# Queueing the state-space scan's decay exponentials behind the attention's score exponentials on ScalarE

## The chip, the cores and the metric

The kernel runs on one core of one Trainium2 chip. The metric is the device time of one execution in microseconds (us). A core has five engines that work side by side, each through its own queue and in that queue's order: TensorE (PE in the profile; PEld is its weight load), VectorE (DVE), ScalarE (ACT), GpSimd (POOL) and SyncE (SP), which here issues the DMAs.

## The reference, cut to what matters

Four residual steps follow one another for each of four batches of 512 rows. The first is a state-space block (a scan over 512 positions for 512 channels with 16 states each), the second a quantised gated feed-forward, the third a cross attention with 16 heads and 512 keys, the fourth four small experts.

```python
def step(state, xs):                                   # the scan, over positions
    d_t, B_t, C_t, u_t = xs
    dA = jnp.exp(d_t[..., None] * A)                   # 512 channels x 16 states
    state = state * dA + (d_t * u_t)[..., None] * B_t[:, None, :]
    y_t = jnp.einsum('ben,bn->be', state, C_t)
    return (state, y_t)
...
scores = jnp.einsum('bqhd,bkhd->bhqk', q, k) * scale   # the attention
attn = jax.nn.softmax(scores, axis=-1)
out = jnp.einsum('bhqk,bkhd->bqhd', attn, v)
...
x = x + jnp.tanh(g_xattn[0]) * _L0_xattn_ref(ctx_1024, _layernorm(x), ...)   # state-space block
x = x + jnp.tanh(g_ffn[0]) * _L0_ffn_ref(_layernorm(x), ...)                 # feed-forward
x = x + jnp.tanh(g_xattn[1]) * _L1_xattn_ref(_layernorm(x), ctx_1024, ...)   # attention
x = x + jnp.tanh(g_ffn[1]) * _L1_ffn_ref(_layernorm(x), ...)                 # experts
```

## The kernel before, in words

**Two streams.** Batch 0 runs its state-space block and its feed-forward alone. After that the kernel gives out two streams side by side: the attention of batch b, head by head, and `layer0(b + 1)`, which is the state-space block (`scan`) and then the feed-forward (`bitnet`) of the next batch. The main loop (L1300 to L1341) has ten slots for each head. In every slot it gives out a piece of the attention of up to three neighbouring heads; and it adds 0.5 to a counter while the scan is being given out (0.8 in the feed-forward), and gives out one piece of `layer0` whenever the counter passes one. So one head goes with five pieces of the scan. `LEADS` says how many heads before its own attention the `layer0` of a batch starts: 16 for batch 1, 17 for batches 2 and 3.

**The scan.** For one batch it has two halves (t0 = 0 and 2), each with 16 states n, each with two channel tiles t: 64 steps. One step is:

- ScalarE writes `dA`, the exponential of delta times A, into a PSUM tile (L652). The tile is one of four in the pool `pss`; two of the four are the accumulators `py` of this half, so two are left for `dA`.
- GpSimd multiplies `du` by `bc`, the row of B that a DMA (L646) has spread over the partitions, into `h` (L186). It does not need `dA`.
- VectorE scans over the positions (L659) and, in six of eight steps, multiplies by `cc` (L660); in the other two VectorE scans (L662) and GpSimd multiplies.
- TensorE adds `h` into `py` by four transposing matmuls (L627).

A piece of the scan is the two steps of one n. At n = 4 of the first half `scan` stands still until `finish(b - 2)` has been given out, because the tile for x of batch b is one of two (L637 to L640).

**The attention.** Each head and each of its four row blocks has scores `ps` (TensorE, L252), their maximum `nmx` (VectorE, L951), its scaling (ScalarE, L963, with `rqs` from GpSimd), and the exponential `pr` (ScalarE, L971). `softmax` gives out two of these exponentials at a time and keeps the last in `mark[0]`; `hl`, the transposed `pT` and the weighted sum `pav` come after it.

**Who sets the order.** When the program is built, a scheduler puts the instructions of each engine in the order in which they will be queued. It takes, by its own estimate of times, the earliest given out of those that are ready. `tc.issue_after(ins)` adds an edge of order: instructions given out inside it are queued behind `ins` on the same engine. It adds no semaphore. The kernel has it already around the staging of weights (`filler`, L1204).

**Where the exponentials stand.** There are 256 score exponentials and 256 exponentials of delta A, each kind in the order given out. Following the loops gives, for each exponential of delta A, how many score exponentials had been given out before it. The table sets this beside the times at which the trace has them (start, us):

| batch, half, n, t | score exponentials given out | it ran at | the last of those ran at |
|---|---|---|---|
| 1, first, 4, 0 | 10 | 397.9 | 396.9 |
| 1, second, 0, 0 | 22 | 477.9 | 513.4 |
| 1, second, 15, 1 | 34 | 577.2 | 589.2 |
| 2, first, 3, 1 | 58 | 759.2 | 749.9 |
| 2, first, 4, 0 | 68 | 762.6 | 812.4 |
| 2, second, 0, 0 | 80 | 866.4 | 895.6 |
| 2, second, 15, 1 | 92 | 957.3 | 973.4 |
| 3, first, 3, 1 | 122 | 1143.2 | 1198.3 |
| 3, first, 4, 0 | 132 | 1144.3 | 1239.1 |
| 3, first, 15, 1 | 140 | 1206.8 | 1295.9 |
| 3, second, 0, 0 | 144 | 1286.6 | 1318.6 |
| 3, second, 15, 1 | 156 | 1372.2 | 1393.0 |

In the trace 168 of the 192 exponentials of delta A of batches 1 to 3 run ahead of the score exponential named in the third column: 47 of batch 1, 57 of batch 2, 64 of batch 3. Score exponentials 1 to 64 are the attention of batch 0, 65 to 128 that of batch 1, and so on.

Of the kernel before, what the change touches and what calls it, by code (L numbers as in the profile page):

```python
# [34 lines left out]
AF = mybir.ActivationFunctionType  # L35
# [75 lines left out]
def flamingo_kernel(  # L111
# [8 lines left out]
    nc = tc.nc  # L120
# [11 lines left out]
    def psum(pool, name, tag="m", bufs=None):  # L132
        if tag == "a":
            role = name.rstrip("_0123456789")
            if pool is psa and role in LAST_PSS and name[len(role)] == str(B - 1):
                return psum(pss, name)
            tag = ATAG.get(role, "m")
            bufs = ABUF[tag]
        kw = {} if bufs is None else {"bufs": bufs}
        return pool.tile([P, 512], F32, tag=tag, name=name, **kw)  # L140
# [12 lines left out]
    def midt(shape, dtype, name, tag):  # L153
        if tag in wider:
            pool, bufs = wider[tag]
            return pool.tile(shape, dtype, tag=f"m{tag}", name=name, bufs=bufs)
        return mid.tile(shape, dtype, tag=tag, name=name, bufs=MIDS[tag])
# [19 lines left out]
    def load_x(b):  # L177
        x_sb[b] = xpool.tile([P, T, L], F32, tag="x", name=f"x{b}", bufs=2)
        nc.sync.dma_start(x_sb[b], x[b].rearrange("(p t) f -> p t f", t=T))
# [5 lines left out]
    def pool_mult(out, a, b):  # L185
        nc.gpsimd.tensor_tensor(out, a, b, ALU.mult)  # L186

    def row_stats(xr, name, gain=1.0, res=None):

        st = sm(6, f"bst{name[0]}", f"bst{name}", 2)  # L190
        nc.vector.bn_stats(st, xr)
        mv = sm(2, f"mv{name[0]}", f"mv{name}")
        nc.vector.bn_aggr(mv, st)
        var = sm(1, f"var{name[0]}", f"var{name}")
        nc.vector.tensor_scalar(var, mv[:, 1:2], EPS, gain**-2, ALU.add, ALU.mult)
        if res is None:
            res = sm(2, f"rst{name[0]}", f"rst{name}")
        rsqrt(res[:, 0:1], var)
        nc.vector.scalar_tensor_tensor(res[:, 1:2], mv[:, 0:1], -1.0, res[:, 0:1], ALU.mult, ALU.mult)
        return res  # L200

    def normed(xr, stats, name, tag="v"):
        xn = midt([P, L], F32, f"xn{name}", tag)
        if name[0] in NRMD:
            nc.vector.tensor_scalar(xn, xr, stats[:, 0:1], stats[:, 1:2], ALU.mult, ALU.add)
        else:
            nc.scalar.activation(xn, xr, AF.Identity, bias=stats[:, 1:2], scale=stats[:, 0:1])
        return xn
# [275 lines left out]
    A = const.tile([P, T, DS], F32, name="A")  # L484
# [30 lines left out]
    def transposed(pool, src, name, g=None):  # L515

        ps = psum(pool, name).rearrange("p (t e) -> p t e", t=T)
        for t, s in enumerate(src):
            nc.tensor.transpose(ps[:, t, :], s[:, g::T], ident)
        return ps[:, : len(src), :]  # L520
# [85 lines left out]
    def scan(b, of_8=DVE_OF_8, G=2, y_tile=lambda name: psum(pss, name), between=lambda n, ins: None):  # L606
        delta, du, ud_d, bd = fronts[b]
        sz_d = dram.tile([P, T, L], F32, tag="szd", name=f"szd{b}", bufs=2)

        def silu_z(t):  # L610

            xt = x_sb[b]
            w = normed(xt[:, t, :], row_stats(xt[:, t, :], f"z{b}{t}", 0.5), f"z{b}{t}")
            th = midt([P, L], F32, f"zth{b}{t}", "t")
            nc.scalar.activation(th, w, AF.Tanh)
            nc.vector.scalar_tensor_tensor(w, th, 1.0, w, ALU.add, ALU.mult)
            return w

        for t0 in range(0, T, G):
            gs = T // G
            ys = [y_tile(f"py{b}{t0}{i}").rearrange("p (g t e) -> p g t e", g=gs, t=G) for i in range(G)]

            def add(src, t, first, last):
                for g in range(T):
                    nc.tensor.matmul(  # L627
                        ys[g // gs][:, g % gs, t, :], src[:, g::T], ident, is_transpose=True,
                        start=first and t == 0 and g % gs == 0, stop=last, skip_group_check=True,
                    )  # L630

            uds, szs = [], []
            for t in range(G):
                uds.append(midt([P, L], F32, f"udr{b}{t0}{t}", "t"))
                nc.sync.dma_start(uds[t], ud_d[:, t0 + t, :])
            for n in range(DS):
                if n == 4 and x_sb[b] is None:  # L637
                    while b >= 2 and estats[b - 2] is None:
                        yield
                    load_x(b)  # L640
                if n == SZR and t0 > 0:
                    for t in range(t0, t0 + G):
                        szs.append(midt([P, L], F32, f"szr{b}{t}", "v"))
                        nc.sync.dma_start(szs[-1], sz_d[:, t, :])
                bc = midt([P, L], F32, f"bc{b}{t0}_{n}", "g")
                nc.sync.dma_start(bc, bd[n, :].partition_broadcast(P))  # L646
                cc = midt([P, L], F32, f"cc{b}{t0}_{n}", "g")
                nc.sync.dma_start(cc, bd[DS + n, :].partition_broadcast(P))
                for t in range(G):
                    nm = f"{b}{t0}{t}_{n}"  # L650
                    dA = psum(pss, f"dA{nm}")
                    last = nc.scalar.activation(  # L652
                        dA, delta[t0 + t], AF.Exp, scale=A[:, t0 + t, n : n + 1]
                    )
                    h = midt([P, L], F32, f"h{nm}", "v")
                    pool_mult(h, du[t0 + t], bc)

                    if (G * n + t) % 8 in of_8:
                        nc.vector.tensor_tensor_scan(dA, dA, h, 0.0, ALU.mult, ALU.add)  # L659
                        nc.vector.tensor_tensor(h, dA, cc, ALU.mult)  # L660
                    else:
                        nc.vector.tensor_tensor_scan(h, dA, h, 0.0, ALU.mult, ALU.add)  # L662
                        pool_mult(h, h, cc)
                    add(h, t, n == 0, n == DS - 1)
                    if n == 2:
                        add(uds[t], t, False, False)
                between(n, last.ins)
                yield

            xt = x_sb[b]  # L670
            if t0 == 0:
                szs = [silu_z(t) for t in range(T)]
                for t in range(G, T):
                    nc.sync.dma_start(sz_d[:, t, :], szs[t])
            for g in range(T):
                if g % gs == 0:
                    acc = midt([P, gs, G, P], F32, f"acc{b}{t0}{g}", "t")
                    nc.scalar.copy(acc, ys[g // gs])
                ps = transposed(pss, szs[:G], f"psz{b}{t0}{g}", g)
                a = acc[:, g % gs]  # L680
                nc.vector.tensor_tensor(a, a, ps, ALU.mult)
                xv = xt[:, g, :].rearrange("q (p e) -> q p e", e=T)[:, :, t0 : t0 + G]
                nc.vector.scalar_tensor_tensor(
                    xv, a.rearrange("q e p -> q p e"), tg[:, 0:1], xv, ALU.mult, ALU.add
                )
                yield
# [511 lines left out]
    mark = [None]  # L1198
# [10 lines left out]
    with tc.tile_pool(name="pro", bufs=1) as pro, tc.tile_pool(name="psp", bufs=4, space=PSUM) as psp:  # L1209
# [26 lines left out]
        def between(n, ins):  # L1236

            if n < 0:
                for _ in range(4):
                    next(side)  # L1240
            for _ in range(2 if 0 <= n < SIDE1 else 0):
                with tc.issue_after(ins):
                    next(side, None)

        run(front(0, inp, between))
        run(scan(0, range(7), 4, iter_ps, between))
        wider.clear()
        for _ in side:
# [34 lines left out]
    def layer0(b):  # L1283

        in_bitnet[0] = False
        if b == 1:
            yield from front(1)
        yield from scan(b)
        in_bitnet[0] = True
        nxt = front(b + 1) if b + 1 < B else iter(())  # L1290
        for k, _ in enumerate(bitnet(b)):
            yield
            if k % NEXT == NEXT - 1:
                next(nxt, None)
        for _ in nxt:
            yield


    n = B * NH
# [114 lines left out]
```

## Time and profile before

| what | value |
|---|---|
| three runs | 2026.92, 2029.95, 2033.11 us; median 2029.95 us |
| the profiled execution | 2033.82 us, its span 2032.0 us |
| granted TensorE clock, mean over the span | 0.877 |
| busy in the span | PE 1634.5, DVE 1536.9, ACT 1328.6, POOL 937.3 us |
| exponentials of delta A, batch 1 | first half 370.0 to 458.0, second 477.9 to 577.2 us |
| batch 2 | first half 737.6 to 831.0, second 866.4 to 957.3 us |
| batch 3 | first half 1118.1 to 1206.8, second 1286.6 to 1372.2 us |
| feed-forward of batches 1, 2, 3: last addition to x (L802) | 747.7, 1132.5, 1528.5 us |
| attention of batches 0 to 3: first and last score exponential | 340.8 to 788.8, 802.3 to 1230.9, 1233.5 to 1590.3, 1602.4 to 1967.7 us |

The times in the table are starts of instructions in one profiled execution, from the start of its span. Busy time is the time in which an engine had work; no engine is busy all the time, and which one is full changes from stretch to stretch. The three runs lie within 6.2 us of each other.

### The profile page before, as it was taken

The page shows a single profiled execution, that of the slowest core. Times are in us where ns is not written, and L with a number is a line of the kernel's source. Part 1 is how long each engine was busy: PE and PEld are TensorE (multiplying, and loading weights), DVE is VectorE, ACT ScalarE, POOL GpSimd, SP SyncE. Part 2 cuts the span into 40 slices and gives each one's busy share as a digit, 9 for nine tenths or more (in the row PEclk, how much of TensorE's full clock was granted, in tenths as well). Part 3 has the DMA queues.
Part 4 walks back from the last instruction along what each step waited for, and adds up shares of the span by engine and source line. Part 5 has one row for each costly group of instructions (what it writes and reads, how often), then busy time and mean ns, then how long its engine had stood idle before and what let it go on. Part 6 is the DMA issues. An engine that isn't in the chain of part 4 may idle for free. (4 is left out here: it accounts for less than half of the span.)

```text
span 2032.0 us, 27171 instructions
## 1 busy us (share of the span) xinstructions
PE 1634.5 (80%) x8366; PEld 901.1 (44%) x8366; DVE 1536.9 (76%) x2893; ACT 1328.6 (65%) x3121; POOL 937.3 (46%) x931
## 2 busy tenths in 40 slices
PE   4354976667879986779898887788999879798888
PEld 1343322344544444455443554554444445454456
DVE  4898865998998787898986885999764564654654
ACT  5797566765757886465658664756565676766763
POOL 1886112784744268475414782775133431412211
PEclk8555987768889998899999989899999889898989
DMA  7553558687884588775435777676445686866754
GB/s 258 185 161 133 151 158 242 185 228 218 231 214 107 132 216 182 191 177 155 106 87 149 199 180 191 156 170 146 91 103 111 139 228 158 210 160 165 193 138 140
DMA packets 516322, 342.50 MB, mean 169 GB/s; under 512 B 425800, under 2 KB 427976, under 8 KB 510032
## 3 DMA queue, kind: packets, MB, share of 16 engines
q1 hardware_dynamic: 516176, 340.77, 64.2%
q8 instruction: 65, 1.06, 0.2%
q14 instruction: 81, 0.66, 0.1%
HBM read 193.10 MB, written 44.30 MB: 117 GB/s over the span
## 5 line engine op out<-in xcount | busy, mean ns | idle before, releaser
L186 POOL TENSOR_TENSOR h<-u,bc 128x512 f32<-128x512 f32 x256 | 334.7, 1327 | 94.5 <-DMA bc<-bd 43.8
L627 PE MATMUL py<-ident,h 128*128 128x128 f32 x1024 | 201.1, 341 | 123.7 <-DVE h L660 101.9
L252 PE MATMUL ps<-kT,qT 128*128 128x512 f16 x768 | 217.0, 406 | 66.5 <-ACT pr L971 51.9
L652 ACT ACTIVATE dA<-delta,A 128x512 f32<-128x512 f32 x256 | 172.6, 685 | 138.8 <-DVE h L660 103.0
L659 DVE TENSOR_TENSOR_SCAN dA<-dA,h 128x512 f32<-128x512 f32 x200 | 240.8, 1217 | 23.5 <-POOL h L186 15.0
L252 PE MATMUL pav<-pT,v 128*128 128x256 f16 x1536 | 215.7, 297 | 46.2 <-DMA pT<-hl 28.9
L627 PEld LDWEIGHTS py<-ident,h 128*128 128x128 f32 x1024 | 167.6, 214 | 167.7 <-DVE h L660 131.0
L951 DVE TENSOR_REDUCE nmx<-ps 128x1 f32<-128x512 f32 x256 | 172.2, 679 | 54.9 <-PE ps L252 54.6
L971 ACT ACTIVATE pr<-ps,nmx,rqs 128x512 f32<-128x512 f32 x256 | 197.7, 775 | 20.8 <-DVE hl L992 16.6
L992 DVE SCALAR_TENSOR_TENSOR hl<-pr,den,hl 128x512 f16<-128x512 f32 x214 | 185.2, 882 | 33.4 <-ACT hl L989 17.0
L252 PEld LDWEIGHTS <-v 128*128 128x128 f16 x1536 | 161.7, 106 | 103.2 <-issue 44.2
L252 PE MATMUL pq<-axnT,wq 128*128 128x512 f16 x768 | 194.1, 404 | 7.7 <-DMA axnT<-xsa 3.1
L252 PE MATMUL pwo<-wo,oT 128*128 128x512 f16 x768 | 181.1, 386 | 8.6 <-DVE oT L244 3.6
L991 POOL TENSOR_SCALAR hl<-pr,den 128x512 f16<-128x512 f32 x86 | 66.3, 771 | 203.5 <-issue 97.5
L252 PEld LDWEIGHTS <-qT 128*128 128x128 f16 x768 | 77.8, 104 | 156.4 <-issue 88.6
L183 POOL TENSOR_TENSOR rqs<-ssq,mhalf 128x4 f32<-128x4 f32 x64 | 68.4, 1068 | 161.9 <-ACT ssq L940 149.0
L252 PEld LDWEIGHTS <-cT 128*128 128x128 f16 x768 | 79.1, 106 | 128.8 <-issue 61.7
L660 DVE TENSOR_TENSOR h<-dA,cc 128x512 f32<-128x512 f32 x200 | 133.7, 677 | 2.5 <-PE py L627 0.5
L252 PEld LDWEIGHTS <-wq 128*128 128x128 f16 x768 | 80.1, 105 | 108.3 <-issue 36.0
L252 PE MATMUL pk<-wk,cT 128*128 128x512 f16 x384 | 110.1, 432 | 19.9 <-DMA wk<-dwk 11.9
L252 PEld LDWEIGHTS <-oT 128*128 128x128 f16 x768 | 74.8, 100 | 100.6 <-issue 10.6
L989 ACT ACTIVATE hl<-pr,den 128x512 f16<-128x512 f32 x128 | 91.8, 717 | 36.3 <-DVE den L978 28.6
(386 smaller groups left out, 3478.2 us busy)
## 6 DMA issues: line engine op xcount, KB each, us to landing
bc<-bd SPq DMA_DIRECT2D x112, 256.0 KB
cc<-bd SPq DMA_DIRECT2D x112, 256.0 KB
wq<-dwq SPq DMA_DIRECT2D x64, 256.0 KB
wo<-dwo SPq DMA_DIRECT2D x64, 256.0 KB
w<-w3d SPq DMA_DIRECT2D x12, 1024.0 KB
de<-hle SPq DMA_DIRECT2D x9, 1024.0 KB
lw<-de SPq DMA_DIRECT2D x18, 512.0 KB
wk<-dwk SPq DMA_DIRECT2D x16, 512.0 KB
```

Of the source, the lines that this page charges most:

```text
L183: nc.gpsimd.tensor_tensor(res, arg, mhalf[:, : arg.shape[1]], ALU.pow)
L186: nc.gpsimd.tensor_tensor(out, a, b, ALU.mult)
L252: nc.tensor.matmul(ps, l, r, start=first and i == 0, stop=last and i == n - 1)
L627: nc.tensor.matmul(ys[g // gs][:, g % gs, t, :], src[:, g::T], ident, is_transpose=True, start=first and t == 0 and g % gs == 0, stop=last ...
L652: last = nc.scalar.activation(dA, delta[t0 + t], AF.Exp, scale=A[:, t0 + t, n : n + 1])
L659: nc.vector.tensor_tensor_scan(dA, dA, h, 0.0, ALU.mult, ALU.add)
L660: nc.vector.tensor_tensor(h, dA, cc, ALU.mult)
L951: nc.vector.tensor_reduce(nmx[:, c : c + 1], ps, AX.X, ALU.max, negate=True)
L971: mark[0] = nc.scalar.activation(pr, scs[c], AF.Exp, bias=nmx[:, one], scale=rqs[:, one], accum_out=den[:, c - c0 : c - c0 + 1],).ins
L989: nc.scalar.activation(hl[:, c, 0], prs[c], AF.Copy, scale=den[:, one])
L991: nc.gpsimd.tensor_scalar(hl[:, c, 0], prs[c], den[:, one], 1.0, ALU.mult, ALU.mult)
L992: nc.vector.scalar_tensor_tensor(hl[:, c, 1], prs[c], den[:, one], hl[:, c, 0], ALU.mult, ALU.subtract)
```

## The change

In batches 1 to 3 every exponential of delta A is given out inside `tc.issue_after(mark[0])`. It is queued on ScalarE behind the last score exponential that had been given out by then: by the table's second column, the exponential of batch 2, first half, n = 4 comes behind score exponential 68. Nothing is added or removed: no instruction, no semaphore, no tile. Batch 0, whose scan runs before any attention, keeps its order.

```diff
                     dA = psum(pss, f"dA{nm}")
-                    last = nc.scalar.activation(
-                        dA, delta[t0 + t], AF.Exp, scale=A[:, t0 + t, n : n + 1]
-                    )
+
+                    with nullcontext() if b == 0 or mark[0] is None else tc.issue_after(mark[0]):
+                        last = nc.scalar.activation(
+                            dA, delta[t0 + t], AF.Exp, scale=A[:, t0 + t, n : n + 1]
+                        )
                     h = midt([P, L], F32, f"h{nm}", "v")
                     pool_mult(h, du[t0 + t], bc)
```

## The prediction, made before the change was run

> **What bounds the kernel now.** I read the page first, then the busy time by stretches, the groups of the scan's lines, the waits by engine, and last the timeline of ScalarE around the exponentials. The page:
>
> ```profile
> span 2032.0 us, 27171 instructions
> PE 1634.5 (80%) x8366; PEld 901.1 (44%) x8366; DVE 1536.9 (76%) x2893; ACT 1328.6 (65%) x3121; POOL 937.3 (46%) x931
> ```
>
> No engine fills the span; ScalarE, whose order changes, is at 65%. So the gain or loss must come from idle time of TensorE and VectorE. The windows view shows in which stretch which of the two is full (columns: length, busy us of PE, PEld, DVE, ACT and POOL with their instructions, TensorE's granted clock, DMA share, GB/s):
>
> ```profile
> 740.00:820.00 80.00, 57.87 (x325) 37.76 (x324) 69.17 (x94) 56.58 (x146) 67.94 (x60) 0.89 0.85 183
> 840.00:860.00 20.00, 13.39 (x64) 7.53 (x63) 11.31 (x28) 9.41 (x27) 6.92 (x9) 0.78 0.84 203
> 860.00:960.00 100.00, 82.82 (x453) 53.13 (x451) 93.11 (x132) 63.02 (x161) 66.71 (x58) 0.91 0.66 169
> 1000.00:1100.00 100.00, 100.00 (x465) 43.29 (x464) 80.44 (x174) 66.25 (x144) 24.64 (x35) 1.00 0.38 97
> 1118.00:1200.00 82.00, 69.49 (x378) 43.27 (x377) 72.94 (x100) 54.30 (x126) 64.53 (x57) 0.92 0.78 194
> 1200.00:1280.00 80.00, 62.72 (x327) 35.53 (x324) 48.06 (x98) 43.14 (x119) 35.24 (x38) 0.91 0.73 174
> 1300.00:1380.00 80.00, 66.76 (x387) 43.41 (x386) 76.56 (x104) 46.48 (x113) 54.70 (x47) 0.96 0.78 186
> 1530.00:1590.00 60.00, 51.66 (x273) 26.93 (x271) 30.97 (x55) 41.09 (x127) 28.53 (x29) 0.96 0.55 120
> ```
>
> Where scan and attention run together (860 to 960, 1300 to 1380) VectorE is full: 93 and 96%. In the feed-forward (1000 to 1100) TensorE is full. Around the start of the next attention nothing is: 840 to 860 and 1200 to 1280 have VectorE at 57 and 60% with no scan in them, because the first half of the scan has ended and its second has not begun.
>
> ```profile
> L627 PE MATMUL py<-ident,h 128*128 128x128 f32 x1024 | 201.1, 341 | 123.7 <-DVE h L660 101.9
> L652 ACT ACTIVATE dA<-delta,A 128x512 f32<-128x512 f32 x256 | 172.6, 685 | 138.8 <-DVE h L660 103.0
> L659 DVE TENSOR_TENSOR_SCAN dA<-dA,h 128x512 f32<-128x512 f32 x200 | 240.8, 1217 | 23.5 <-POOL h L186 15.0
> L660 DVE TENSOR_TENSOR h<-dA,cc 128x512 f32<-128x512 f32 x200 | 133.7, 677 | 2.5 <-PE py L627 0.5
> ```
>
> One step of the scan costs VectorE 1.217 + 6/8 x 0.677 = 1.725 us. ScalarE idles 138.8 us in front of `dA`, mostly for VectorE to free the `dA` tile: `dA` is early, not late. The waits view of ScalarE and of VectorE (total us, times, longest):
>
> ```profile
> ACT dA L652 <- DVE h L660: 103.0, 62, 6.0
> ACT nmx L963 <- DVE nmx L951: 34.1, 39, 2.2
> ACT dA L652 <- DVE h L662: 33.7, 22, 6.1
> ACT nmx L963 <- POOL rqs L183: 27.5, 22, 2.9
> ACT pr L971 <- DVE hl L992: 16.6, 14, 4.7
> ```
>
> ```profile
> DVE dA L659 <- ACT dA L652: 8.1, 12, 1.3
> ```
>
> VectorE's scan waited for ScalarE 8.1 us in all. And what stands behind an early `dA`, in ScalarE's timeline:
>
> ```profile
> 811.44 0.69 ACT L652 ACTIVATE dA<-delta,A 128x512 f32<-128x512 f32 x1 [2.90 <-DVE h L662]
> 812.07 0.28 ACT L963 ACTIVATE nmx<-nmx,rqs 128x1 f32<-128x1 f32 x1
> 812.38 0.78 ACT L971 ACTIVATE pr<-ps,nmx,rqs 128x512 f32<-128x512 f32 x1
> ```
>
> The score exponential comes only after 2.90 us in which ScalarE waited for the scan.
>
> **The change part by part.** No instruction is added: the edge costs nothing by itself, and no DMA or GpSimd instruction carries it. What moves is when 168 exponentials, and the scan steps behind them, run. Five terms, on the profiled execution.
>
> *Batch 3, first half.* 24 exponentials (n = 4 to 15) ran from 1144.3 to 1206.8; each now waits at least for score exponential 132, which ran at 1239.1. Their scan work is 24 x 1.725 = 41.4 us of VectorE. It moves into 1200 to 1280, where VectorE idles 80 - 48.06 = 31.9 us; at the 96% of 1300 to 1380 it can take 28.7 us of that, so 12.7 us prolong the stretch. Where they were, the attention now runs nearly alone. From 1124.5 to 1198.3 it did ten exponentials in 73.8 us. Alone it does 15 in the 60 us of 1530 to 1590 (4.0 us each) or 15 in 1206.8 to 1286.6 (5.3 us): ten take 40 to 53 us, and the eight steps of n = 0 to 3 that stay add 8 x 4 x 0.286 = 9 us of transposes (0.286 is the median row of L627). That saves 12 to 25 us. Net -12 to +1; I take the middle, -6.
>
> *Batch 2, first half.* 17 exponentials ran from 762.6 to 811.4, ahead of number 68 at 812.4. They move 17 x 1.725 = 29.3 us of VectorE behind it. The hole at 840 to 860 takes 20 - 11.31 = 8.7 us; 20.6 remain. The attention's nine exponentials from 757.0 to 812.4 took 55.4 us, alone 36 to 48: saved 7 to 19. Net +2 to +14. GpSimd is 85% busy at 740 to 820, and its `h` products stand in front of the attention's first norms and copies, so the change relieves that start too: I take +5, the lower part.
>
> *Batch 1 and the ends of the scans.* Batch 1 leads by at most six score exponentials; its last `dA` ran 12.0 us before the one it must now follow. The feed-forward may end as much later, and the next attention prepares 4 us after it: 0 to +12. By then the attention stands further on by the same work, so I take +2. The second halves of batches 2 and 3 lead by 16.1 and 20.8 us at their ends; their feed-forwards end at 1132.5 and 1528.5, 98 and 62 us before the attention beside them ends, which hides it: 0. Without that cover it would cost these 16 and 21 us.
>
> *The score exponentials come out from behind the scan.* TensorE waits in front of `ps` for `pr` 8.5 us in 430 to 600, 11.1 in 737 to 835, 2.4 in 860 to 960 and 6.4 in 1110 to 1210: 28.4 us. Bounds 0 to -28; a `dA` given out earlier still stands in front of the next `pr`, so I take half, -14.
>
> *The scan comes in behind waiting exponentials.* Queued behind a `pr` or its `nmx`, a `dA` inherits their waits. The waits view of ScalarE over the five stretches of the scan (370 to 577, 737 to 831, 866 to 957, 1118 to 1207, 1286 to 1372) gives for both lines 16.0, 2.4, 2.4, 3.2 and 6.2 us, in sum 30.2. Queued behind the `dA`: VectorE's scan, TensorE's transposes, GpSimd's products once their six tiles are full. Bounds 0 to +30. Two `dA` tiles and 117.8 us of `dA` waiting for VectorE in the same stretches say that most of it is slack: +2.
>
> The rule against this change is in the Trainium skill, "TensorE: Matmul & The Clock Gate", section on the array's architecture: ScalarE's queue is strictly first in, first out, so an instruction that is ready cannot pass one that is not. The 2.90 us above agree with it; taken alone it would set the last term at its upper end, and the total would be +17 in place of the -11 that follows from the rows.
>
> Sum: -6 + 5 + 2 - 14 + 2 = -11 us. The profiled execution took 2033.82 us, 3.87 over the median; 2033.82 - 11 - 3.87 = 2019.
>
> **The rivals.** *Starved scan, slower.* In the scan's stretches VectorE is 93 to 96% full, so a wait that reaches it is paid. Place: ScalarE's queue; price: the 30.2 us of inherited waits, of which the attention's own VectorE work (30.97 of 60 us when alone, half) covers half: +15; and the relief fails, as each `pr` now has another burst of `dA` in front of it: 0 for -14. Sum -6 + 5 + 2 + 15 = +16: 2046. It decides once the waits that reach VectorE exceed the relief of the score exponentials by over 5 us. For it: VectorE's fullness. Against: 8.1 us of waits for `dA` now.
>
> *A shift and nothing else.* The same work meets the same full engines, relief and inherited waits cancel: -6 + 5 + 2 = +1, 2031. For it: the feed-forward stretches are full of TensorE either way.
>
> That the edge binds nothing is ruled out by the 168 exponentials that now run ahead of their mark.
>
> **How the numbers follow.** The forecast has 0.53, the starved scan 0.35, the shift 0.12. A measurement can tell about 0.3% (6 us) from no change. Faster 0.53, same 0.12, slower 0.35. Forecast's own range: low ends -12 + 2 + 0 - 28 + 0 = -38, 1992, and up to -6, 2024. To hold 8 in 10 with the rival and its bounds (+16 with +9 if batch 2 costs 14): 1994 to 2056.
>
> **What would show it.** Right: no exponential of delta A starts before its mark; scan steps of batch 3 at 1200 to 1280 with VectorE over 85% there; ScalarE's wait of `dA` for VectorE falls from 136.7 us to under 100; the attention of batch 2 starts before 1225. Wrong: VectorE's wait for `dA` grows from 8.1 us beyond 20; the attention of batch 1 starts no earlier than 802 and its first heads take longer; the feed-forward of batch 1 ends over 12 us later.

## The result and the profile after

The changed kernel is slower. In comparisons on the same chip it takes 2040.25 us (median of 20 runs, 2024.23 to 2046.69), the kernel before 2030.74 us (20 runs, 2023.01 to 2041.18). The ratio is 1.0042, with an interval of 1.0027 to 1.0057: a loss of some 9 us. The prediction said 2019 us and "faster"; the time lies in its range, the direction was wrong.

A loss of 9 us is smaller than what executions of one and the same program differ by (22 us from the lowest to the highest above). The profiled execution of after took 2031.86 us, 8 us less than its median; that of before took 2033.82 us, 3 us more than its median. So the spans of the two pages show no loss at all. The change was therefore profiled a second time; that execution took 2040.09 us (span 2038.3 us) and is called "the second profile" below. A reading counts only where both profiles, or several kernels, have it. The granted TensorE clock, mean over the span, was 0.884 and 0.889 in these two and 0.877 before, so a lower clock is not the cause of the loss.

The page of after, engines and groups of the scan (busy us and mean ns; then the idle time in front and who ended most of it). The lines of the scan stand two lower in the file than before: L652, L659, L660 and L662 are now L654, L661, L662 and L664.

```profile
span 2030.1 us, 27143 instructions
PE 1623.6 (80%) x8366; PEld 892.1 (44%) x8366; DVE 1542.7 (76%) x2893; ACT 1330.5 (66%) x3123; POOL 942.8 (46%) x931
L627 PE MATMUL py<-ident,h 128*128 128x128 f32 x1024 | 199.8, 338 | 132.6 <-DVE h L662 109.6
L654 ACT ACTIVATE dA<-delta,A 128x512 f32<-128x512 f32 x256 | 170.3, 684 | 95.4 <-DVE h L662 76.3
L661 DVE TENSOR_TENSOR_SCAN dA<-dA,h 128x512 f32<-128x512 f32 x200 | 239.9, 1217 | 29.1 <-ACT dA L654 18.4
```

The work is the same: counts, busy time and the 1.217 us of one scan, but for two more loads of ScalarE's activation table (38 in place of 36, 1.28 us each, in both profiles). Lag 8 below has the same 38 and is faster than the kernel before, so they alone do not make the loss. ScalarE idles 95.4 us in front of `dA` in place of 138.8, so `dA` comes later, as the change says. No exponential of delta A runs ahead of its mark (168 did before).

The waits view of after, whole span:

```profile
PE py L627 <- DVE h L662: 109.6, 67, 14.8
...
ACT dA L654 <- DVE h L662: 76.3, 42, 6.0
...
PE ps L252 <- ACT pr L973: 50.1, 36, 5.4
ACT nmx L965 <- DVE nmx L953: 49.8, 45, 6.5
...
DVE dA L661 <- ACT dA L654: 18.4, 15, 4.2
```

ScalarE's wait for VectorE in front of `dA` is 76.3 + 16.8 (the other line of `h`) = 93.1 us, before 136.7. In exchange VectorE's wait for `dA` rose from 8.1 to 18.4 us, ScalarE's wait for the row maxima (`nmx`) from 34.1 to 49.8, and TensorE's wait of `ps` for `pr` fell only from 51.9 to 50.1. The second profile has 18.5 us for VectorE and 48.7 for TensorE.

The windows view of after, in four of the stretches shown before:

```profile
740.00:820.00 80.00, 56.36 (x294) 31.38 (x293) 52.45 (x83) 49.67 (x126) 51.76 (x48) 0.84 0.70 156
...
1118.00:1200.00 82.00, 68.73 (x352) 35.58 (x351) 57.31 (x94) 61.50 (x145) 47.05 (x45) 0.98 0.74 183
1200.00:1280.00 80.00, 61.60 (x323) 34.68 (x323) 59.08 (x109) 43.41 (x110) 48.51 (x48) 0.94 0.68 177
1300.00:1380.00 80.00, 63.67 (x353) 39.74 (x352) 74.30 (x103) 47.77 (x113) 50.07 (x43) 0.93 0.71 185
```

VectorE's hole at 1200 to 1280 is fuller by 11.0 us (48.06 to 59.08, 74%), but a new hole has opened ahead of it: at 1118 to 1200 VectorE fell from 72.94 to 57.31, and at 740 to 820 from 69.17 to 52.45. The second profile has 58.14, 57.09 and 48.51 in these three. TensorE did not fill either of the new holes: 56.36 us of 80 where it had 57.87, and 68.73 of 82 where it had 69.49 (57.65 and 71.64 in the second profile). The idle time of VectorE moved from behind the first piece of the scan to the place in front of it.

Now the stages. A1 is the start of score exponential 65, the first of batch 1's attention; the next columns are how long it took from there to number 129 (first of batch 2), to 193 (first of batch 3), and to 256 (the last). Starts of instructions in the traces, us:

| kernel | A1 | 65 to 129 | 129 to 193 | 193 to 256 |
|---|---|---|---|---|
| before | 802.3 | 431.2 | 368.9 | 365.3 |
| after | 798.7 | 422.0 | 386.7 | 358.6 |
| second profile of the change | 808.6 | 425.8 | 384.3 | 357.0 |

The attention of batch 1 got shorter by 5 to 9 us and that of batch 2 longer by 15 to 18. The next section takes the change apart to see which batch's edge does which.

### The profile page after: what moved, and what is told of

It reads as the page before. It is cut to its first block, busy times and chain, and to the rows that moved or that the text cites. A ratio compares the mean times of both kernels' runs of the same rounds, so it can differ in the third digit from the quotient of the medians.

```text
span 2030.1 us, 27143 instructions
## 1 busy us (share of the span) xinstructions
PE 1623.6 (80%) x8366; PEld 892.1 (44%) x8366; DVE 1542.7 (76%) x2893; ACT 1330.5 (66%) x3123; POOL 942.8 (46%) x931
## 5 line engine op out<-in xcount | busy, mean ns | idle before, releaser
L186 POOL TENSOR_TENSOR h<-u,bc 128x512 f32<-128x512 f32 x256 | 340.5, 1348 | 107.8 <-PE py L627 60.9
L252 PE MATMUL ps<-kT,qT 128*128 128x512 f16 x768 | 215.2, 400 | 62.3 <-ACT pr L973 50.1
L661 DVE TENSOR_TENSOR_SCAN dA<-dA,h 128x512 f32<-128x512 f32 x200 | 239.9, 1217 | 29.1 <-ACT dA L654 18.4
L252 PE MATMUL pav<-pT,v 128*128 128x256 f16 x1536 | 209.1, 287 | 40.0 <-DMA pT<-hl 21.5
L654 ACT ACTIVATE dA<-delta,A 128x512 f32<-128x512 f32 x256 | 170.3, 684 | 95.4 <-DVE h L662 76.3
L994 DVE SCALAR_TENSOR_TENSOR hl<-pr,den,hl 128x512 f16<-128x512 f32 x214 | 195.3, 931 | 29.1 <-ACT hl L991 15.2
L252 PE MATMUL pq<-axnT,wq 128*128 128x512 f16 x768 | 201.9, 416 | 18.1 <-DMA axnT<-xsa 8.1
L252 PEld LDWEIGHTS <-v 128*128 128x128 f16 x1536 | 156.0, 103 | 98.2 <-issue 43.9
L662 DVE TENSOR_TENSOR h<-dA,cc 128x512 f32<-128x512 f32 x200 | 133.0, 675 | 1.4 <-PE py L627 0.5
L965 ACT ACTIVATE nmx<-nmx,rqs 128x1 f32<-128x1 f32 x256 | 69.7, 293 | 77.0 <-DVE nmx L953 49.8
L991 ACT ACTIVATE hl<-pr,den 128x512 f16<-128x512 f32 x128 | 92.0, 719 | 42.2 <-DVE den L980 34.1
```

What stands on the lines that cost most here:

```text
L252: nc.tensor.matmul(ps, l, r, start=first and i == 0, stop=last and i == n - 1)
L654: last = nc.scalar.activation(dA, delta[t0 + t], AF.Exp, scale=A[:, t0 + t, n : n + 1])
L965: nc.scalar.activation(nmx[:, one], nmx[:, one], AF.Copy, scale=rqs[:, one])
L991: nc.scalar.activation(hl[:, c, 0], prs[c], AF.Copy, scale=den[:, one])
L994: nc.vector.scalar_tensor_tensor(hl[:, c, 1], prs[c], den[:, one], hl[:, c, 0], ALU.mult, ALU.subtract)
```

## The experiments

Times are medians; the ratio is to the kernel before on the same chip, with its 95% interval. It is estimated from the runs of both kernels and is not the quotient of the two medians, from which it differs by up to 0.2%. A "part" keeps the edge in some batches only; its edit is the condition in the `with` line.

**Batch 1 alone.**

```diff
-with nullcontext() if b == 0 or mark[0] is None else ...
+with nullcontext() if b != 1 or mark[0] is None else ...
```

> The edge in batch 1 alone; batches 2 and 3 keep their order. Starved scan (the exponential of delta A inherits the waits of the score exponentials, in proportion to the waits that stand in the stretches of before: 16.0 of 30.2 us lie in batch 1): about half of the +9.5 us of the whole change, +5 us. Hold-out (the cost sits where n = 4 to 15 of the first half waits for the next attention, which batch 1 does not have): 0 us, within 3. Lost relief alone (nothing is added, the gain just does not come): 0 us.

Measured: 2022.69 us, ratio 0.999 [0.9968, 1.0012]: no loss.

**Batch 2 alone** (`b != 2` in the same place).

> The edge in batch 2 alone. Starved scan: 4.8 of 30.2 us of waits lie here, +1 to +2 us. Hold-out: 17 scan steps leave the start of attention 1, where VectorE then has nothing, and 20.6 us of scan work find no idle time later: +5 to +14 us, the larger part of the whole. My own third term: +5 us.

Measured: 2027.87 us, 1.001 [0.9995, 1.0025]: no more than 0.25%.

**Batch 3 alone** (`b != 3`).

> The edge in batch 3 alone. My first term: -6 us (bounds -12 and +1), since the scan fills the idle time at the start of attention 2. Starved scan: 9.4 of 30.2 us of waits lie here, +3 us. Hold-out: the scan comes late by up to 89 us against before and its feed-forward ends later: 0 to +8 us.

Measured: 2026.89 us, 1.0013 [0.9994, 1.0032].

Of 2030 us the ratios make -2, +2 and +3: the three parts add up to about +3, the whole loses 9. None of the parts gains what was forecast for the whole. By their intervals the sum is uncertain by some 7 us, so these three runs do not yet show that the loss lies outside the parts; the pairs below do.

**Only the pieces that stood behind the standstill for x**, the first halves of batches 2 and 3 from n = 4.

```diff
+with tc.issue_after(mark[0]) if b >= 2 and t0 == 0 and n >= 4 else nullcontext():
```

> The edge only on the 48 exponentials of n = 4 to 15 of the first halves of batches 2 and 3. Hold-out: the whole +9.5 us, within 4. Starved scan: only a quarter of the edges bind, +2 to +3 us. By my first two terms: -6 + 5 = -1 us.

Measured: 2029.84 us, 1.0029 [1.0012, 1.0045]. **The edge everywhere but there:**

```diff
+with nullcontext() if b == 0 or mark[0] is None or (b >= 2 and t0 == 0 and n >= 4) else ...
```

> The edge everywhere in batches 1 to 3 except on the 48 exponentials of n = 4 to 15 of the first halves of batches 2 and 3. Hold-out (the cost sits at those 48, which alone gave +0.29%): within 3 us of before. Starved scan (each binding edge costs): 144 edges against 48, so +6 us or more.

Measured: 2037.18 us, 1.0051 [1.0032, 1.007]. The division that the prediction rested on (first halves of batches 2 and 3 against the rest) does not separate gain from loss: the first side loses 6 us, though it has no edge in batch 1, and the other side loses as much as the whole. **The whole change once more:**

> The whole change once more, on this chip beside the others: +0.42% (interval 0.27 to 0.57) of the first comparison, +8.5 us.

Measured: 2039.19 us, 1.0057 [1.0038, 1.0077]. The result repeats. Next, two batches at a time.

**Batches 2 and 3** (`b < 2` takes no edge).

> The whole edge in batches 2 and 3, batch 1 as before. Late feed-forward (in the profiles of the change the feed-forward of batch 1 ends 3 to 12 us later, and the next attention starts about 50 us after that end whatever the order was, so there is no slack): without the edge in batch 1 that is gone, +2 to +5 us, the sum of the two parts run alone (+2.0 and +2.6). Starved scan: 13 to 15 us of VectorE's waits in the change lie mostly in batches 2 and 3 (11.9 of 14.5), so +7 us.

Measured: 2030.92 us, 0.9998 [0.9977, 1.0018]. **Batches 1 and 2** (`b in (0, 3)` takes none).

> The whole edge in batches 1 and 2, batch 3 as before. Batch 1 alone gave -0.10%, batches 2 and 3 together -0.02%, all three +0.42 to +0.57%, so the loss needs batch 1 and another. Unfilled start (batch 1's edge ends its feed-forward later, and batch 2's edge takes from the start of attention 1 the scan that filled it: VectorE at 740 to 840 is 87 us busy of 100 with batch 1's edge alone, 70 with both): +8 to +12 us. Sum of the parts run alone: 0 us. Order and nothing else: anything within 16 us.

Measured: 2046.2 us, 1.0097 [1.0073, 1.0121]: 20 us, where the two parts alone make 0. **Batches 1 and 3** (`b in (0, 2)` takes none).

> The whole edge in batches 1 and 3, batch 2 as before. Unfilled start: the scan of batch 2 still fills the start of attention 1, so within 4 us of before. Sum of the parts: +1 us. Order and nothing else: anything within 16 us.

Measured: 2033.41 us, 1.003 [1.0012, 1.0048], 6 us. So the edges of batches 1 and 2 together make a loss that neither makes alone, and with batch 3's edge added about half of it is gone again (20 us without it, 9 to 12 with it). The pair 1, 3 is not clear: its 6 us lie within the uncertainty of the sum of its parts, about +1. A loss without any edge in batch 1 exists too, the 6 us of the first halves of batches 2 and 3 above, although the full edge in both batches loses nothing; no run here explains it. The stages of these kernels, one profile each; the last column is the profiled execution less the median of its kernel, us:

| edge in | A1 | 65 to 129 | 129 to 193 | 193 to 256 | VectorE's waits for `dA` | result | profile |
|---|---|---|---|---|---|---|---|
| none | 802.3 | 431.2 | 368.9 | 365.3 | 8.1 | | +3.1 |
| 1 | 823.0 | 417.7 | 364.6 | 362.3 | 8.8 | 0.999 | +10.9 |
| 2 | 796.1 | 436.8 | 369.0 | 358.6 | 10.1 | 1.001 | -4.5 |
| 3 | 801.9 | 415.1 | 384.7 | 361.9 | 10.8 | 1.0013 | +0.1 |
| 2, 3 | 797.0 | 419.1 | 380.7 | 365.2 | 15.5 | 0.9998 | -5.6 |
| 1, 3 | 813.0 | 409.0 | 383.9 | 359.2 | 12.7 | 1.003 | -3.6 |
| 1, 2 | 800.6 | 443.8 | 372.4 | 360.7 | 16.2 | 1.0097 | -2.8 |

Three things can be read from it. *Batch 3's edge* makes the stage 65 to 129 shorter and the stage 129 to 193 longer by about as much, in whatever company: -16 and +16 alone, -18 and +12 with batch 2, -9 and +19 with batch 1, and, from the row "1, 2" to the two profiles of the whole change, -18 to -22 and +12 to +14. What attention 1 gains while the scan of batch 3 is held back, attention 2 pays back; the reading is that the scan then runs beside it. *Batch 1's edge alone* starts attention 1 late by 20.7 us, but 13.5 of them are made up in the next stage and the rest by the last exponential (1967.6 and 1967.7 us). This profile is the slowest execution of its kernel, so the 20.7 us are less certain than the order. *Batch 2's edge*, added to batch 1's, makes the stage 65 to 129 longer, 443.8 us in place of 417.7. Most of that is only that attention 1 starts 22.4 us earlier: in the pair it is not late at all (800.6, before 802.3). Against the kernel before the stage is 12.6 us longer, where batch 2's edge alone makes it 5.6 longer, and the feed-forward of batch 2 ends at 1164.6, before at 1132.5, with batch 1's edge alone at 1136.0 and with batch 2's at 1149.5. The windows view shows where TensorE falls behind. Its two stretches are the start of batch 2's scan and the whole of batch 2's scan and feed-forward; first the kernel before:

```profile
740.00:840.00 100.00, 76.54 (x419) 48.96 (x418) 88.95 (x133) 64.50 (x163) 77.24 (x70) 0.90 0.83 194
740.00:1100.00 360.00, 306.40 (x1566) 169.98 (x1565) 306.35 (x551) 229.79 (x573) 196.83 (x195) 0.92 0.62 151
```

the whole change (first profile):

```profile
740.00:1100.00 360.00, 294.60 (x1525) 164.91 (x1525) 301.70 (x540) 224.21 (x572) 206.38 (x201) 0.91 0.61 149
```

batch 1 alone:

```profile
740.00:840.00 100.00, 75.37 (x406) 45.68 (x405) 87.33 (x119) 71.41 (x167) 82.15 (x71) 0.88 0.80 184
740.00:1100.00 360.00, 305.72 (x1553) 168.46 (x1551) 310.12 (x558) 234.58 (x566) 201.39 (x199) 0.91 0.62 154
```

batch 2 alone:

```profile
740.00:840.00 100.00, 75.54 (x386) 44.13 (x384) 69.90 (x118) 60.41 (x159) 59.81 (x57) 0.88 0.76 176
740.00:1100.00 360.00, 301.31 (x1575) 168.85 (x1573) 301.59 (x542) 230.41 (x595) 201.43 (x200) 0.94 0.64 154
```

and batches 1 and 2:

```profile
740.00:840.00 100.00, 73.51 (x373) 41.57 (x374) 69.95 (x117) 63.32 (x163) 64.04 (x60) 0.88 0.73 181
740.00:1100.00 360.00, 294.12 (x1512) 165.48 (x1512) 300.48 (x529) 219.60 (x563) 204.66 (x200) 0.91 0.60 148
```

With batch 1's edge alone VectorE is 87% busy at 740 to 840, nearly as before (89%): batch 2's scan fills the time in which attention 1 starts late. Held back too, it leaves VectorE at 70%. That by itself is not the loss, for batch 2's edge alone leaves it at 70% as well. But TensorE is busy for only 294.12 us by 1100, 11.6 less than with batch 1 alone and 7.2 less than with batch 2 alone. The whole change has 294.60 (and 292.61 in the second profile), the kernel before 306.40.

If the lateness of A1 costs nothing by itself, a harder delay of batch 1 alone must cost nothing either. In this run the edge goes to the exponential third from last: `marks` is a list of all marks, and "lag 2" means the one two before the last.

```diff
+with nullcontext() if b != 1 or len(marks) <= 2 else tc.issue_after(marks[-1 - 2]):
...
+                marks.append(mark[0])
```

> Two back, in batch 1 alone. With two back everywhere the feed-forward of batch 1 ended 27 us later than before while the attention beside it stood 16 us further on, and the time was +2.0%. Late feed-forward: attention 1 starts about 11 us later than before here too, and the time is +10 to +25 us. If what counts is the total of waits and not this end: a third of the +41 us, +14 us; if batches 2 and 3 make it: within 4 us.

Measured: 2027.71 us, 0.9988 [0.9972, 1.0005], although A1 stood at 827.8 and the feed-forward of batch 1 ended at 780.0 (before 747.7), 32 us late.

**Slack.** The same edge in batches 1 to 3, but to an exponential some way behind the last:

```diff
+with nullcontext() if b == 0 or len(marks) <= LAG else tc.issue_after(marks[-1 - LAG]):
```

Lag 2:

> Each exponential of delta A of batches 1 to 3 is queued behind the score exponential given out two before the last one: the pair before, half a head earlier. Starved scan (VectorE's waits for the exponential of delta A in the scan's stretches rose from 4.2 us before to 14.5 and 15.4 us in the two profiles of the whole change): the pair before has long run, so these waits fall to 4 to 7 us and the time falls by about 10 us from the whole change, to within 4 us of before. Late scan (the cost is that the scan stands later against the attention, by up to 20 score exponentials): two of twenty change little, the time stays at +7 to +10 us.

Lag 4:

> The same with four, one head. Starved scan: VectorE's waits are those of before, and the time is between before and the -0.84% of eight, -2 to -12 us. Late scan: +5 to +8 us, on a straight line from the whole change (+0.5%) to none.

Lag 8:

> Each exponential of delta A of batches 1 to 3 is queued behind the score exponential that had been given out eight before the last one, two heads earlier. Most edges then bind little or not: by the table of before, those that still do are the first half of batch 3 and a part of the first half of batch 2. Starved scan: 0 to +2 us. Hold-out: half of its cost, since number 132 becomes 124 and 68 becomes 60: 0 to +3 us. If any queueing behind score exponentials relieves them, as my fourth term said: below before by some us.

Lag 16:

> The same with sixteen, four heads. By the trace of before only exponentials of the first half of batch 3 ran more than sixteen ahead, by 17 to 20. Starved scan and late scan: within 4 us of before. If the gain at eight comes from holding back the first half of batch 3: a small part of it, -1 to -5 us. If any change of the order moves the time by this much: anything between -16 and +16 us.

| lag | 0 (the change) | 2 | 4 | 8 | 16 |
|---|---|---|---|---|---|
| time, us | 2040.25 | 2071.18 | 2027.57 | 2011.45 | 2018.71 |
| ratio | 1.0042 | 1.0203 | 1.0003 | 0.9916 | 0.9948 |
| interval | 1.0027, 1.0057 | 1.0181, 1.0225 | 0.9984, 1.0022 | 0.9895, 0.9936 | 0.993, 0.9966 |
| VectorE's waits for `dA`, us | 18.4 | 25.1 | 24.2 | 8.4 | 12.7 |
| 129 to 193, us | 386.7 | 401.3 | 384.4 | 367.5 | 364.5 |

Lag 8 is 16 us faster than the kernel before, and 28 us faster than the whole change on the same chip (2039.19). It lets an exponential of delta A run up to eight score exponentials ahead of the mark that the change gives it. The windows view of lag 8:

```profile
740.00:1100.00 360.00, 309.34 (x1599) 168.30 (x1599) 311.70 (x566) 237.50 (x594) 201.32 (x202) 0.95 0.65 156
```

TensorE has been busy for 309.34 us by 1100, more than in the kernel before. This measure does not order the kernels, though; lag 4, which loses nothing, has less than before:

```profile
740.00:1100.00 360.00, 298.38 (x1542) 165.70 (x1541) 304.79 (x545) 228.19 (x566) 196.23 (x196) 0.92 0.63 151
```

In lag 8 the stage 65 to 129 is 415.8 us, short as with batch 3's edge, and the stage 129 to 193, 367.5 us, does not grow for it. Lag 2 shows that a looser edge is not always a better one. **Lag 8 in batch 3 alone** (`b != 3 or len(marks) <= 8`):

> Eight back, in batch 3 alone. The first half of batch 3 ran 16 to 20 score exponentials ahead, and with eight it ended at 1244 in place of 1207 us, beside the start of attention 2, where VectorE had idled. If the -16 us of eight are made there: -12 to -16 us. If batch 2 (17 exponentials 8 to 10 ahead) makes them: within 4 us of before.

Measured: 2028.4 us, 1.0002 [0.9988, 1.0015]: the gain of lag 8, like the loss of lag 0, is not made by the last batch alone.

**Another order around the edge.** The standstill for x moved from n = 4 to the last n, with the whole change, so that more of the scan is given out early:

```diff
-if n == 4 and x_sb[b] is None:
+if n == DS - 1 and x_sb[b] is None:
```

> The whole change, and the standstill for the tile of x moved from n = 4 to n = 15 of the first half. The exponentials n = 4 to 14 then follow score exponentials 60 to 68 and 124 to 132, not 68 to 76 and 132 to 140: up to two heads sooner, while the edge stands on all 192. Hold-out: its +6 us goes, 0 to +3 us against before. Starved scan: stays at +8 us, as every exponential is still queued.

Measured: 2048.67 us, 1.0111 [1.0077, 1.0144], with 8.1 us of VectorE's waits for `dA`, no more than before. And six pieces of the scan to a head in place of five, with the change and without it:

```diff
-RATE_S = 0.5
+RATE_S = 0.6
```

> The whole change, with six instead of five pieces of the scan given out per head (rate 0.6). Every exponential of delta A is still queued behind the last score exponential given out, but that one is now earlier: the last of batch 1 follows number 28 to 30 and not 34. Late feed-forward: layer0 of batch 1 ends as early as before, and against the next kernel, the same rate without the edge, the loss is 0 to +3 us. Starved scan: the waits are inherited as before, +8 us against the next.

> The kernel before with rate 0.6: the partner of the run above. In before most exponentials of delta A run when their tiles come free, ahead of where they are given out, so giving them out earlier should move little: within 6 us of before under either theory. More than that would say that the order found by the scheduler moves the time by as much as the change does.

Measured: 2040.22 us with the edge, 1.0058 [1.0037, 1.0078]; 2020.41 us without it, 0.9953 [0.9934, 0.9972]. The edge loses at this rate too, by 19.8 us, more than at 0.5; VectorE's waits for `dA` are 9.7 us with it and 7.4 without.

## Why the prediction was wrong

Five terms, on the profile of before, gave -6 + 5 + 2 - 14 + 2 = -11; measured were +9. Two steps failed. The first is the fourth term, the relief of the score exponentials: without it the sum is +3, no gain, and the three batches taken singly, which should have brought it, add up to about +3. The second is adding the costs of batches 1 and 2 as if they were independent: the pair was put at 7 us and loses 20. Each term in turn, then the sum.

**Batch 3, first half (-6): the mechanism was right alone, its bill too small.** With batch 3's edge alone the attention beside the held scan did get faster: the ten exponentials from number 112 to 122, from which the term was worked out, took 55.2 us in place of 73.8, 18.6 saved, within the 12 to 25 predicted. In the two profiles of the whole change they took 70.4 and 70.7: 3 us saved. With batch 2's edge alone they took 92.1. There the feed-forward of batch 2 ends at 1149.5, in the whole change at 1158.1 and 1169.2, before at 1132.5, so it runs beside more of these ten; the prediction took the attention there to be nearly alone. Attention 2 started at 1220.7 in the first profile and at 1234.4 in the second, before at 1233.5. The prolonging was put at 12.7 us from "at the 96% of 1300 to 1380 it can take 28.7 us of that", and VectorE took 11.0 more at 1200 to 1280, not 28.7. The scan of batch 3 began late and ran beside attention 2, which paid 12 to 19 us. The net of the part alone is +0.13% (+3 us).

**Batch 2, first half (+5): right as far as it goes.** Alone it measures +2 us (interval -1 to +5), at the end of its bounds. That it relieves the start of attention 1 agrees with the trace: 796.1 in place of 802.3.

**Batch 1 (+2): the second step that failed.** "By then the attention stands further on by the same work, so I take +2" holds for batch 1 alone, even if its feed-forward ends 32 us late. It does not hold beside batch 2's edge. The two costs were worked out apart, each with the other edge absent, and added: 7 for the pair, where the pair measures 20. A reading that suggests itself is that batch 2's free scan covers the late start of attention 1, and that the second term had taken this cover away. The traces do not bear it out as it stands: in the pair attention 1 starts at 800.6, not late, and the time is lost after that, in a stage 65 to 129 that is 12.6 us longer than before. The feed-forward of batch 2, too, ended 25.6 and 36.7 us later in the two profiles of the whole change, where the prediction had 16 us and took them to be hidden.

**Relief of the score exponentials (-14): the first step that failed.** In the stretches with scan (340 to 610, 735 to 1005, 1110 to 1425) TensorE's waits of `ps` for `pr` fell from 39.4 us to 36.1 and 34.1 in the two profiles: -3 to -5. The prediction counted half of its 28 us as gained, because a `dA` given out earlier still stands in front of the next `pr`; the wait stayed nearly whole. Nor does the time follow this wait one for one: with batch 1's edge alone it fell from 51.9 to 36.5 us over the span (one profile), and the time by 2 us, which is within its noise. At 0.6 pieces the wait rose instead, from 34.3 to 49.2 us over the span.

**Inherited waits (+2): under-sized.** VectorE's waits for `dA` rose by 10.3 us, a third of the upper bound of 30, and not by 2. The direction agrees with the rule in the Trainium skill, "TensorE: Matmul & The Clock Gate", section on the array's architecture, that ScalarE's queue is strictly first in, first out; the rule names no price for the wait.

**The rivals.** With the measured sizes of the last two terms the sum would be -6 + 5 + 2 - 3 + 10 = +8, about the loss, and the starved scan, with its point of decision at 5 us (10.3 - 3.3 = 7), would seem proved. The runs say otherwise. Batches 2 and 3 together have 15.5 us of these waits and lose nothing, lag 4 has 24.2 and loses nothing, the late x has 8.1, as before, and loses 1.1%, and at 0.6 the waits rise by 2.3 us for a loss of 19.8. So these waits are real, but no kernel's time follows them; that this sum comes near the loss is luck. These waits are from one profile of each kernel. The shift (+1) fits each part alone and the pair 2, 3, but not the whole.

**The stated signs.** Those for "right": nothing ahead of its mark (so it was); ScalarE's wait under 100 us (93.1); attention 2 before 1225 (1220.7, but 1234.4 in the second profile); VectorE over 85% at 1200 to 1280 (74 and 73%: failed). Those for "wrong": VectorE's waits beyond 20 us (18.4 and 18.5: not reached); attention 1 no earlier than 802 (798.7 and 808.6) and its first heads longer (its first 15 exponentials took 99.6 and 96.6 us, before 93.3); feed-forward of batch 1 over 12 us later (2.8 and 12.2). Two of these three, and the start of attention 2, change sides from one profile to the other. The premise that no instruction is added missed the two more table loads.

**What stays open.** Shown by times: the edges of batches 1 and 2 lose together what neither loses alone, and batch 3's edge takes part of it back. Seen in the profiles: with both of these edges, in the pair and in the two profiles of the whole change, TensorE is 12 to 14 us less busy between 740 and 1100 than before; and batch 3's edge moves time from one attention to the next. How batches 1 and 2 lose together stays open. Less busy time of TensorE is not enough for it, since lag 4 has 8.0 us less than before and loses nothing. The order alone, without any edge, moved the time by 8 us (0.6 pieces), about what the change does, and these profiles show no reason why lag 2 loses 44 us against lag 4, whose waits of VectorE are as long (25.1 and 24.2 us). Nor is it explained why the pair 1, 3 loses 6 us; its TensorE is busy for 309.80 us between 740 and 1100, so it does not fall behind there. Which batches make the gain of lag 8 was not tried beyond batch 3 alone.

## What to carry to other kernels

An edge that only fixes an order adds nothing to the program, but it takes slack out of a pipeline of several streams, and costs that were worked out place by place need not add up: here two places lost 20 us together and nothing apart. When a change sits in several places, work out and test them in pairs, not only one by one. A wait that shrinks in the profile is not a gain until a run shows it as time: here one shrank by 15 us, while the time moved by 2, within the noise. If a queue is to be held back, leave some slack and try a few amounts: behind the last exponential the kernel lost 0.4%, two behind it 2.0%, eight behind it gained 0.8%. What one stage gains the next may pay back, so compare the lengths of stages over several profiles before explaining a difference below the spread of executions.

## What the runs showed that was not expected

Executions of one program on one core spread over 22 us (2024 to 2047, 1.1%), with a profile of after 8 us below its median. The time is not monotone in the slack: +0.42, +2.03, +0.03, -0.84 and -0.52% at lags 0, 2, 4, 8 and 16. And a delay of 32 us in the feed-forward of batch 1 (780.0 against 747.7) cost nothing that 12 runs could show, when the batch behind it was free to move.
